# A cross-attention and mixture-of-experts block: short runs in memory, weight reloads one step ahead, a running sum on VectorE, values' product two steps behind the scores

## The chip, the cores and the metric

The kernel runs on one core of a Trainium2 chip. A core has TensorE (PE in the profile; the loading of its stationary operand is PEld), VectorE (DVE), ScalarE (ACT), GpSimd (POOL) and SyncE (SP), and 16 DMA engines that all queues share. SP and POOL issue the DMAs here. The metric is the device time in microseconds; smaller is better. The figure for a kernel is the median of its timed runs; one further execution is recorded by the profiler.

## The reference

Four sequences (b = 0 to 3) of 512 rows by 512 columns go through two blocks.

```python
# block 1: per sequence, on layernormed rows
query, key = ctx @ Wq.T + bq, ctx @ Wk.T + bk
x = x + layernorm(x) @ softmax(query @ key.T).T
# block 2, attention: 16 heads of 128 columns
h = rmsnorm(z, ln1_w)                       # z = layernorm(x)
q, k, v = h @ wq, h @ wk, h @ wv
attn = softmax(causal(q @ k.T / sqrt(128)))
z = z + (attn @ v) @ wo
# block 2, experts: 16 experts of width 352, the 6 best of each row, and a shared one of width 704
t = rmsnorm(z, ln2_w)
cw = top6(softmax(t @ gate_w.T)), renormalised
routed = sum over e of cw[:, e] * ((silu(t @ eg[e].T) * (t @ eu[e].T)) @ ed[e].T)
shared = (silu(t @ sg_w.T) * (t @ su_w.T)) @ sd_w.T
out = x + z + routed + shared
```

## The kernel before, in words

**Precision.** Every product keeps about fp32 accuracy by splitting each operand into an fp16 high and low part (`split`, L72: one ScalarE copy and one VectorE subtraction) and adding three fp16 matmuls (`mm3`, L80; the lines L83, L86 and L87 are its three matmuls wherever it is called). A matmul streams up to 512 columns.

**Stages.** Block 1 for b = 0 and most of b = 1 comes first (about 0 to 85 us of the trace). Then the main loop (L780) goes over 64 heads, one head to a step n, in the order of `path` (L768): two neighbouring sequences take the same pair of heads after each other, so that one load of weights serves both. Block 1 of the later sequences is spread over the steps (`step`, L837 to L841). The loop ends near 1020 us; the shared expert, the 16 routed experts and the gathering of their rows follow.

**A step n of the loop.** `queries` (L637) makes q and k of head n, `values` (L623) makes v for a pair of heads, `scores` (L654) makes the four row blocks of the causal scores with 128, 256, 384 and 512 columns. Each block goes to VectorE (mask and maximum, L671), ScalarE (exponential with sum, L673), VectorE (reciprocal), and then through `split` into the tile `pn`. A DMA transpose on SP's queue (`flip`, L90 and L680) turns `pn` into the tile `pt` in SBUF. `attend` (L682) multiplies `pt` with v. It is called for head n - LAG, and LAG is 1. `project` (L695) multiplies the result with wo when a pair of heads is through, and adds to x2. When the last pair of a sequence is through, `route1` to `route3` (L485, L532, L587) choose the experts; the rows are scattered to the experts' places by 24 indirect DMAs a sequence on POOL's queue (`scatter`, L464). `pace` (L456) is a small POOL copy that reads the newest result of `attend` or of the shared expert, so that POOL doesn't run ahead with its scatters.

**Where order is decided.** The functions are called in the order above, but a scheduler places the instructions on each engine; a tile pool with a fixed number of buffers makes a new tile wait for the old one's last reader. Within one engine, POOL and SP among them, instructions run in the order so placed, and a waiting instruction holds up all behind it.

**Weights.** Sequence 0's pass loads fp32 weights, splits them, uses them, and writes the fp16 pair to DRAM scratch (`wqk_d`, `wv_d`, `wo_d`; 512 KB each, 4 KB to a partition). Later passes reload from there: `fetch` (L407) issues the reload on POOL's queue (L414) in the step in which the weights are used. The tile for a weight has 2 buffers.

**Tiles for the transposed scores.** `pt` is 8 blocks of 512 columns (8 KB a partition), of which the causal triangle fills 20 blocks of 128; the pool `ht` holds two. In `attend` the block row k of v meets the columns from 128k on:

```python
for k in range(NT):
    mm3(pv[:, k * P:], [(vt[:, k, 0, hl], vt[:, k, 1, hl], pt[:, 2 * k, k * P:],
                         pt[:, 2 * k + 1, k * P:])], start=k == 0, stop=k == NT - 1)
```

Of the kernel before, what the change touches and what calls it, by code (L numbers as in the profile page):

```python
# [24 lines left out]
G = 8  # L25
# [24 lines left out]
LAG = 1  # L50
# [5 lines left out]
def xattn_moe_block_kernel(ctx: ExitStack, tc: tile.TileContext, x, xT, ctxT, wqkx, bqk, ln1, ln2,  # L56
# [23 lines left out]
    def mm3(o, terms, start=True, stop=True, hold=None):  # L80
# [7 lines left out]
        return ins  # L88

# [42 lines left out]
    hid_d = [dram.tile([P, NT, D], F32, name=f"hid_d{b}") for b in range(B)]  # L132
    x1_d = [dram.tile([P, NT, D], F32, name=f"x1_d{b}") for b in range(B)]
    wqk_d = [dram.tile([P, 2048], F16, name=f"wqk_d{h}") for h in range(H)]
    wv_d = [dram.tile([P, 8 * GW], F16, name=f"wv_d{g}") for g in range(G)]
    wo_d = [dram.tile([P, 2 * HG * D], F16, name=f"wo_d{g}") for g in range(G)]
    xs_d = dram.tile([ROWS, 2 * D], F16, name="xs_d")
    r_d = [dram.tile([P, NT, D], F32, name=f"r_d{b}") for b in range(B)]
# [30 lines left out]
    ht = bpool("ht")  # L169
# [9 lines left out]
    def ctx_load(b):  # L179
        t = stg.tile([P, 1024], F32, tag="st", name="ct32").rearrange("p (c s) -> p c s", c=CC)  # L180
        feed(b).dma_start(t, ctxT[b])
        return t
# [21 lines left out]
    def xattn(b):  # L204
        ct32 = ctx_load(b) if b else ct0

        def turned(j):
            t = (stg if b else wg).tile([P, 1024], F32, tag="st" if b else "wo", name="xT32")
            feed(b).dma_start(t, xT[b, j])
            return t  # L210
# [5 lines left out]
        if b == 0:  # L216
            nc.sync.dma_start(ln1b, ln1.partition_broadcast(P))
            for nm, src in (("wqk0", wqk[0]), ("wv0", wv[0])):
                t = vp.tile([P, NT, 2, GW], F16, tag="vt", name=f"{nm}_st")
                early_st[nm] = t.rearrange("p t a d -> p (t a d)").bitcast(F32)  # L220
                nc.sync.dma_start(early_st[nm], src)
# [20 lines left out]
        def wide(nm):  # L242
            return (ap_ if b else ht).tile([P, 2 * C, S], F16, tag=nm if b else "pt", name=f"{nm}{b}")
# [88 lines left out]
        for t in range(NT):  # L332
# [6 lines left out]
            q.dma_start(x1_d[b][:, t, :], xv)  # L339
# [15 lines left out]
            if b >= 2:  # L355
                q.dma_start(hid_d[b][:, t, :], hd)
# [37 lines left out]
    def shared_pool():  # L394
# [5 lines left out]
        for j in range(0, C * 2 * SI, 1024):  # L400
            pieces.append((shw[:, :, j:min(j + 1024, C * 2 * SI)], sgu[:, j:min(j + 1024, C * 2 * SI)]))
        for j in range(0, 6 * D, 1024):
            pieces.append((sdw[:, :, j:j + 1024], sd[:, j:j + 1024]))

    held, partner, seen = {}, {}, set()

    def fetch(b, g, pool, tag, n, src, scr, nm):  # L407
        if held.get(nm, (None,))[0] == (b, g):
            return held.pop(nm)[1]
        w = pool.tile([P, 2, n], F16, tag=tag, name=f"{nm}_{b}")  # L410
        if (b, g) in partner:
            held[nm] = partner[b, g], w
        if nm in seen:
            nc.gpsimd.dma_start(w.rearrange("p a n -> p (a n)"), scr)  # L414
# [5 lines left out]
        else:  # L420
            st_ = stg.tile([P, 1024], F32, tag="st", name=f"{nm}_st")
            q = nc.sync if nm == "wqk1" else nc.gpsimd
            ins = q.dma_start(st_[:, :n], src)
# [5 lines left out]
        ins = (nc.sync if nm == "wqk0" else nc.gpsimd).dma_start(scr, w.rearrange("p a n -> p (a n)"))  # L429
# [10 lines left out]
    def shared_weights():  # L440
# [6 lines left out]
        if pieces:  # L447
            dst, src = pieces.pop(0)
            n = src.shape[1]
            st_ = stg.tile([P, 1024], F32, tag="st", name="shst")[:, :n]  # L450
            pin(nc.gpsimd.dma_start(st_, src))
# [842 lines left out]
```

## Time and profile before

| | |
|---|---|
| Median of the timed runs | 1773.08 us (1766.79 to 1774.21, 3 runs) |
| The profiled execution: its own time | 1762.41 us |
| its span from first to last instruction | 1760.7 us |
| mean granted TensorE clock | 0.993 |
| TensorE busy | 1708.6 us, 97% of the span |
| VectorE, ScalarE, GpSimd busy | 63%, 47%, 28% |
| DMA: SP's queue, POOL's queue | 39.9% and 25.5% of 16 engines' span |

The page lists busy times, the granted clock, the DMA queues and the costliest groups of instructions; a row "A <- B: us, times, longest" of the waits says how long engine A stood idle before an instruction and which event ended that. A row of the timeline gives start, duration, engine, line, operation and tiles, and in square brackets the idle time before it. Matmuls overlap, so a matmul's pace is read from the distance between two starts (0.215 us at 512 columns, 0.056 at 128), not from its duration (0.38 us).

### The profile page before, as it was taken

The numbers are of one execution on the slowest core, as the hardware profiler recorded it, in microseconds if no ns is written. First come the engines' busy times: TensorE is split into PE (matmuls) and PEld (weight loads), VectorE is DVE, ScalarE is ACT, GpSimd is POOL, SyncE is SP. The second block draws the span as 40 slices with busy tenths as digits, with TensorE's granted clock in tenths as the row PEclk, the third lists the DMA queues.
The fourth block names the chain that finished last, engine by engine and source line by source line (L and its number), as shares of the span: only waits on it lengthen the run. The fifth ranks groups of instructions, "written<-read, shape, count | busy, mean of one in ns | idle before, by whom it ended". The sixth has DMA issues, their size and how long they took to land. (4 is left out here: it accounts for less than half of the span.)

```text
span 1760.7 us, 27659 instructions
## 1 busy us (share of the span) xinstructions
PE 1708.6 (97%) x9919; PEld 932.9 (53%) x9919; DVE 1116.2 (63%) x2766; ACT 829.3 (47%) x1711; POOL 485.1 (28%) x614
## 2 busy tenths in 40 slices
PE   7899999999998999999999999999999999999998
PEld 3555556565654555556555544455555555555553
DVE  6787877787785676776667647544434344356755
ACT  4565655565643545454445422344544445444431
POOL 5524212240255242121113454300000000034654
PEclk9999999999999999999999999999999999999999
DMA  7787867575687787556547653755554546589866
GB/s 246 181 205 184 225 150 192 122 196 118 138 183 187 163 177 179 120 120 118 111 104 132 140 155 128 247 173 148 150 173 137 154 143 163 154 228 254 221 198 213
DMA packets 392212, 296.24 MB, mean 168 GB/s; under 512 B 334880, under 2 KB 335136, under 8 KB 391296
## 3 DMA queue, kind: packets, MB, share of 16 engines
q1 hardware_dynamic: 353360, 159.87, 39.9%
q0 software_dynamic: 38704, 134.51, 25.5%
q8 instruction: 80, 1.31, 0.3%
q14 instruction: 68, 0.56, 0.1%
HBM read 124.81 MB, written 88.94 MB: 121 GB/s over the span
## 5 line engine op out<-in xcount | busy, mean ns | idle before, releaser
L1169 POOL DMA_INDIRECT yg<-y_d,yrc x96 | 109.9, 1145 | 505.2 <-PE u L87 426.0
L673 ACT ACTIVATE pe<-pe,bnm 128x128 f32<-128x128 f32 (+3 forms) x256 | 142.5, 557 | 161.5 <-DVE bnm L671 161.3
L83 PE MATMUL qk<-hT,wqk 128*128 128x512 f16 (+1 forms) x520 | 196.4, 378 | 9.1 <-DMA wqk<-wqk_d 5.5
L86 PE MATMUL qk<-hT,wqk 128*128 128x512 f16 (+1 forms) x520 | 196.5, 378 | 0.0
L87 PE MATMUL qk<-hT,wqk 128*128 128x512 f16 (+1 forms) x520 | 196.3, 377 | 0.0
L74 DVE SCALAR_TENSOR_TENSOR pn<-pe,brc,pn 128x128 f16<-128x128 f32 (+3 forms) x256 | 148.1, 590 | 21.3 <-ACT pn L73 18.0
L671 DVE CUSTOM_DVE_ANT_0 pe<-sc,causal 128x128 f32<-128x128 f32 (+3 forms) x256 | 117.0, 485 | 66.9 <-PE sc L668 65.9
L73 ACT ACTIVATE pn<-pe,brc 128x128 f16<-128x128 f32 (+3 forms) x256 | 133.5, 553 | 34.1 <-ACT pe L673 17.8
L83 PE MATMUL v<-wv,hT 128*128 128x256 f16 x512 | 139.8, 273 | 0.9 <-DMA hT<-hh 0.9
L87 PE MATMUL v<-wv,hT 128*128 128x256 f16 x512 | 139.7, 273 | 0.0
L86 PE MATMUL v<-wv,hT 128*128 128x256 f16 x512 | 139.7, 273 | 0.0
L83 PE MATMUL g<-xT,wt 128*128 128x384 f16 (+2 forms) x384 | 127.3, 331 | 0.0
L86 PE MATMUL g<-xT,wt 128*128 128x384 f16 (+2 forms) x384 | 127.2, 331 | 0.0
L87 PE MATMUL g<-xT,wt 128*128 128x384 f16 (+2 forms) x384 | 127.2, 331 | 0.0
L1058 ACT ACTIVATE hT_e<-hf 128x384 f16<-128x384 f32 (+3 forms) x96 | 51.1, 532 | 133.6 <-DVE hf L1072 133.2
L83 PE MATMUL y<-dt,hT_e 128*128 128x512 f16 (+1 forms) x288 | 109.4, 380 | 0.0
L87 PE MATMUL y<-dt,hT_e 128*128 128x512 f16 (+1 forms) x288 | 108.9, 378 | 0.0
L86 PE MATMUL y<-dt,hT_e 128*128 128x512 f16 (+1 forms) x288 | 108.9, 378 | 0.0
L73 ACT ACTIVATE qkt<-qk 128x512 f16<-128x512 f32 x128 | 75.1, 587 | 70.7 <-PE qk L87 70.5
L705 DVE SCALAR_TENSOR_TENSOR x<-wo,x 128x512 f32<-128x512 f32 x128 | 87.2, 685 | 33.3 <-PE wo L87 32.9
L467 POOL DMA_INDIRECT xs_d<-h2p,slotu x96 | 98.7, 1028 | 28.3 <-issue 27.1
L74 DVE SCALAR_TENSOR_TENSOR qkt<-qk,qkt 128x512 f16<-128x512 f32 x128 | 87.5, 684 | 18.3 <-ACT qkt L73 15.2
(333 smaller groups left out, 4041.5 us busy)
## 6 DMA issues: line engine op xcount, KB each, us to landing
y_d<-yt SPq DMA_DIRECT2D x96, 256.0 KB, 2.8
est<-in_ew_dram SPq DMA_DIRECT2D x32, 704.0 KB, 6.2
est<-in_ed_dram SPq DMA_DIRECT2D x16, 768.0 KB, 4.7
wqk<-wqk_d POOLq DMA_DIRECT2D x20, 512.0 KB, 5.0
wqk_d<-wqk POOLq DMA_DIRECT2D x15, 512.0 KB, 4.0
wqk_st<-in_wqk_dram POOLq DMA_DIRECT2D x14, 512.0 KB, 6.4
xs_d<-causal POOLq DMA_DIRECT2D x16, 384.0 KB, 5.6
wv<-wv_d POOLq DMA_DIRECT2D x10, 512.0 KB, 5.7
```

The lines of the kernel that those rows point to most:

```text
L73: return (nc.scalar.activation(hi, src, AF.Copy, scale=scale), nc.vector.scalar_tensor_tensor(lo, src, scale, hi, ALU.mult, ALU.subtract))
L74: nc.vector.scalar_tensor_tensor(lo, src, scale, hi, ALU.mult, ALU.subtract))
L83: ins = nc.tensor.matmul(o, lh, rh, start=start and j == 0, stop=False)
L86: nc.tensor.matmul(o, lh, rl, start=False, stop=False)
L87: ins = nc.tensor.matmul(o, ll, rh, start=False, stop=stop and j == n - 1)
L467: ins = nc.gpsimd.indirect_dma_start(out=xs_d, out_offset=bass.IndirectOffsetOnAxis(ap=slotu[:, tt, k:k + 1], axis=0), in_=h2ps[tt], in_of ...
L671: nc.vector.tensor_tensor_reduce(pe, ps[:, :w], causal[:, S - w:], -1.0, 3e38, ALU.add, ALU.min, nm)
L673: nc.scalar.activation(pe, pe, AF.Exp, bias=nm, scale=-1.0, accum_out=sm)
L705: nc.vector.scalar_tensor_tensor(x2[:, t, :], ps, 1.0 / (VS * WS), x2[:, t, :], ALU.mult, ALU.add)
L1058: nc.scalar.activation(hT[:R, ic, :w], hf, AF.Copy)
L1169: nc.gpsimd.indirect_dma_start(out=yg, out_offset=None, in_=src, in_offset=bass.IndirectOffsetOnAxis(ap=idx[:, tt, k:k + 1], axis=0))
```

## The change

1. `LAG` is 2: `attend` of a head is called two steps after its `scores`. The pool `ht` has 3 buffers. The tile `pt` is packed: 20 blocks of 128 columns, so a flip writes one stretch. `attend` goes over pairs of row blocks instead, with 18 matmuls of 256 or 128 columns in place of 12 of 512, 384, 256 and 128. The last two heads are attended in step 64.
2. `fetch` has a mode `early`: after the queries of step n, the reloads of the weights of step n + 1 are issued (q/k and v), and wo's in the step that attends the pair's last head. `pace` is placed behind them.
3. `runs` cuts every plain DMA of those tensors in pieces; the scratch tensors and four inputs are laid out as [piece, partition, run] with runs of 1 KB in scratch and 2 KB in the inputs.
4. The running sum over experts in `route2` (four additions a sequence) goes from GpSimd to VectorE.
5. Around these: block 1 of b = 0 keeps one tile in `hpool` in place of `ht`; steps 1 to 5 take three pieces of b = 1's block 1 instead of steps 0 to 5 two; the early part of the shared expert takes 2 chunks to a tile, and two chunks, one, and three are placed around the last heads.

```diff
-LAG = 1
+RUN = 256
+LAG = 2
...
+    def runs(q, o, i):
+        blocks = [v.rearrange("p (q n) -> p q n", q=w.shape[0]) if len(v.shape) == 2 else v.rearrange("q p n -> p q n")
+                  for v, w in ((o, i), (i, o))]
+        return q.dma_start(*blocks)
...
-    wqk_d = [dram.tile([P, 2048], F16, name=f"wqk_d{h}") for h in range(H)]
+    def rows_d(nm, b):
+        return dram.tile([NT, D // RUN, P, RUN], F32, name=f"{nm}{b}")
+
+    def weights_d(nm, i):
+        return dram.tile([2048 // (2 * RUN), P, 2 * RUN], F16, name=f"{nm}{i}")
...
-    ht = bpool("ht")
+    ht = bpool("ht", LAG + 1)
...
-    def fetch(b, g, pool, tag, n, src, scr, nm):
+    def fetch(b, g, pool, tag, n, src, scr, nm, early=False):
+        if early and nm not in seen or soon.get(nm) and early:
+            return
         if held.get(nm, (None,))[0] == (b, g):
-            return held.pop(nm)[1]
-        w = pool.tile([P, 2, n], F16, tag=tag, name=f"{nm}_{b}")
+            return None if early else held.pop(nm)[1]
+        w = soon.pop(nm, None)
+        if w is None:
+            w = pool.tile([P, 2, n], F16, tag=tag, name=f"{nm}_{b}")
+            if nm in seen:
+                zz["load"] = runs(nc.gpsimd, w.rearrange("p a n -> p (a n)"), scr)
+        if early:
+            soon[nm] = w
+            return
...
-        if "rrs" in zz:
-            after(ins, zz["rrs"])
+        for k in ("rrs", "load"):
+            if k in zz:
+                after(ins, zz[k])
...
-            nc.gpsimd.tensor_tensor(nx[:, :, sft:], cs[:, :, sft:], cs[:, :, :E - sft], ALU.add)
+            nc.vector.tensor_tensor(nx[:, :, sft:], cs[:, :, sft:], cs[:, :, :E - sft], ALU.add)
...
-        pt = pts[b, h] = ht.tile([P, 2 * NT, S], F16, tag="pt", name="pt")
+        pt = pts[b, h] = ht.tile([P, NT * (NT + 1), P], F16, tag="pt", name="pt")
...
-            flip(pt[:, :2 * (t + 1), tl], pn)
+            flip(pt[:, t * (t + 1):(t + 1) * (t + 2), :], pn)
...
-        for k in range(NT):
-            mm3(pv[:, k * P:], [(vt[:, k, 0, hl], vt[:, k, 1, hl], pt[:, 2 * k, k * P:],
-                                 pt[:, 2 * k + 1, k * P:])], start=k == 0, stop=k == NT - 1)
+        for t in range(0, NT, 2):
+            for k in range(t + 2):
+                q = max(k, t)
+                o = pv[:, q * P:(t + 2) * P].rearrange("p (n q) -> p n q", q=P)
+                first = q * (q + 1) + 2 * k
+                phi, plo = (pt[:, first + a:first + a + 2 * (t + 1 - q) * (q + 1) + 1:2 * (q + 1), :] for a in range(2))
+                mm3(o, [(vt[:, k, 0, hl], vt[:, k, 1, hl], phi, plo)], start=k == 0, stop=k == t + 1)
...
-    for n in range(NH + LAG + 1):
+    for n in range(NH + 2):
...
+            if n + 1 < NH:
+                b, h = heads[n + 1]
+                wqk_of(b, h, True)
+                if h % HG == 0:
+                    wv_of(b, h // HG, True)
         m = n - LAG
...
-            for ic in range(3 * (n - NH), 3 * (n - NH) + 3):
...
+            hs0 = chunks(*((3, 6) if n > NH else (0, 2)))
...
-        if 0 <= m < NH:
-            b, h = heads[m]
+        for i in [m] * (0 <= m < NH - LAG) + [NH - 2, NH - 1] * (n == NH):
+            b, h = heads[i]
             attend(b, h)
             if h % HG == HG - 1:
                 ready.append((b, h // HG))
+                wo_of(b, h // HG, True)
+        if n == NH:
+            chunks(2, 3)
...
-            step(1, 2)
+            step(1, 3 * (n > 0))
```

## The prediction, made before the changed kernel had run

> **What bounds the kernel now.** I read the busy shares first, then TensorE's waits, then the timeline around the longest waits and POOL's timeline at the same moments.
>
> ```profile
> span 1760.7 us, 27659 instructions
> ## 1 busy us (share of the span) xinstructions
> PE 1708.6 (97%) x9919; PEld 932.9 (53%) x9919; DVE 1116.2 (63%) x2766; ACT 829.3 (47%) x1711; POOL 485.1 (28%) x614
> ```
>
> TensorE is busy 97% of the span, and its matmuls follow each other at the pace of their columns. So only its pauses can be won, and every pause that the change adds is lost. The waits of the whole run:
>
> ```profile
> engine line waited for: us in total, times, longest us
> PE av L83 <- DMA pt<-pn: 16.9, 10, 3.9
> PE xm L83 <- DMA ptp<-pn: 9.8, 2, 5.8
> PE qk L83 <- DMA wqk<-wqk_d: 5.5, 1, 5.5
> PE u L1081 <- DVE hf L1072: 3.9, 2, 2.1
> PE qk L83 <- DMA hT<-hh: 3.6, 2, 3.2
> ```
>
> The first and third rows lie in the main loop and are what parts 1 and 2 of the change aim at: values waiting for transposed scores, and one q/k weight that came late. The second and fifth belong to the start. Now the late weight on TensorE:
>
> ```profile
> 542.92 0.38 PE L668 MATMUL sc<-qkt,qkt 128*128 128x512 f16 x1
> 548.81 0.61 PE L83 MATMUL qk<-hT,wqk 128*128 128x512 f16 x1 [5.51 <-DMA wqk<-wqk_d]
> 549.21 0.63 PE L86 MATMUL qk<-hT,wqk 128*128 128x512 f16 x1
> 549.64 0.63 PE L87 MATMUL qk<-hT,wqk 128*128 128x512 f16 x1
> 550.07 0.63 PE L83 MATMUL qk<-hT,wqk 128*128 128x512 f16 x1
> ```
>
> After the pause starts are 0.43 us apart where 0.215 is usual: half pace. It lasts to 554.0, which costs 2.6 us more. The same follows the longest wait for scores (3.91 us, ending at 970.0): half pace to 972.8, 1.2 us. No other wait of the loop, the longest of them 2.48 us, is followed by it. On POOL's queue at that time:
>
> ```profile
> 537.35 1.28 POOL L467 DMA_INDIRECT xs_d<-h2p,slotu  x1 [0.30 <-issue]
> 538.93 0.96 POOL L467 DMA_INDIRECT xs_d<-h2p,slotu  x1 [0.30 <-issue]
> 539.89 0.60 POOL L414 DMA_DIRECT2D wqk<-wqk_d  x1
> ```
>
> The reload is issued at 539.89, three microseconds before TensorE wants it, behind ten scatters that POOL had been issuing since 525.7, about 1.27 us each.
>
> **LAG 2 and the packed triangle.** TensorE's columns stay the same: 512 + 384 + 256 + 128 = 1280 before, 2 x 128 + 128 + 3 x 256 + 128 = 1280 after, three matmuls each. Instructions rise from 12 to 18 per head, 384 in all. A 128-column matmul starts 0.056 us after the last and a 256-column one 0.109, so cutting 256 in two costs 3 ns; 384 x 3 ns = **+1 us**. The moving operand now steps over blocks of 128, which the trace has nowhere. It can't gain, as the columns are the same; at worst each block costs like a matmul of its own, 64 x 12 x 3 ns = 2 us. I take nothing, as all rows here go by columns.
>
> For the wait I compare, head by head, two things. The latency from the last 512-column score matmul to the landing of the last flip, in the trace, is 14.5 us in the median and 23.2 at most. The cover is the matmul work that stands in TensorE's order between those scores and the head's first value matmul, columns at 0.422 ns. It is 11.0 to 24.0 us before, under 14.5 in fourteen heads; in the changed order it is 13.2 for the first head, 17.9 for the second, and 19.5 to 40 for all others. With the old latencies only one head past the first falls short, by 0.8 us. I leave 1 us: **16.9 - 1 = 15.9 us gone, and 1.2 of half pace**.
>
> What comes later in its place? Each `attend` moves with its ScalarE and VectorE split, then `project`, behind one more head. Two covers shrink. The time between the end of q/k and the first scores falls to 2.3 to 3.8 us in about twenty heads (4.8 was common); the old q/k latencies (1.4 us usual, up to 6.8 early) laid against it give **+2 us** in two heads, early. The first `project` of heads 2 and 3 gets 1.0 us after its values, against a split of 0.58 + 0.68 us: **+0.5 us**. At the end, the last wo matmul stands 14.9 us before the router's matmuls of sequence 3, against 19.9 before; the chain between (norm, split, four flips) took 18.0, of which the last flip took 7.7 where 2.9 is the median. So 0 to 3.1 us; I take **+1.5**. A flip now also waits for `attend` of three heads ago; no flip is behind that, as the third buffer goes with the longer lag.
>
> **Reloads a step ahead.** In POOL's new order the reload that stalled stands before the ten scatters, and the next one, behind twenty of them, is wanted about 37 us of matmul work later. Buffers are free when it is issued, since the tile's last reader is a head back. So **5.5 + 2.6 us go**. POOL's idle time ahead of L414 (82 us for wo, 58 for q/k), in which all its queue stood, shrinks too; nobody on the critical path had felt it otherwise.
>
> **Short runs.** 71 of POOL's copies go from 128 to 512 runs, 95 from 128 to 256, and SP's likewise at the start. Two costs. First, issue: the one POOL copy of 128 x 4 runs is L215, the usual one L414.
>
> ```profile
> L215 POOL DMA_DIRECT2D xt<-in_x_dram x2: 788/812/837, 136.6 to 347.6; - x2
> L414 POOL DMA_DIRECT2D wqk<-wqk_d x20: 528/546/597, 444.0 to 958.8; - x20
> ```
>
> So 71 x 0.27 = 19 us, and 95 x 0.09 = 9 us if it goes by runs: 28 us of POOL's time over 1000. The Trainium skill ("DMA: Bandwidth & Descriptors", "Anatomy of one DMA") says descriptor generation on this path is small and that many can be emitted before the increment shows; by that the cost is nothing. I take the row. Neither is on the path: POOL is busy 28%, and the reloads now have a head's time. If that cover were gone, each would cost 0.27 us, about 10 us for 40 reloads.
>
> Second, the DMA engines. In the trace a 2 KB packet takes 84 ns and a 4 KB one 159, so 9 ns and 37 ns per KB; four runs of 1 KB would take 183. Then 72 x 128 x 24 ns / 16 = 14 us of each engine, with the 2 KB pieces about 20 us in 1000: 2 points on a DMA share of 0.5 to 0.87. The same page ("Why small descriptors are slow") speaks against the edit more mildly, with some 3 cycles a packet beside 32 for 1 KB: 7% in place of 15%. Both ends are hidden behind flips with 5 us of new slack. Better spread in DRAM could also shorten transfers (4 KB packets of POOL's queue average 217 ns against a median of 159). I take zero, with -3 to +3 us for the start, where loads stand on the path.
>
> **Running sum.** 16 additions leave POOL (0.27 to 0.29 us) for VectorE, where the same size takes 0.155 (L957): 2.5 us on an engine at 63%, in the router's chain, which has a step to spare. Zero. The other rearrangements (tile pools, chunks) keep TensorE's work; b = 1's first value product gets 1 us more of matmuls ahead of its 4 us wait at 72 us: **-1**.
>
> **The sum.** -15.9 - 1.2 - 5.5 - 2.6 - 1 = -26.2; +1 + 2 + 0.5 + 1.5 = +5. Net -21. Against the profiled execution, 1762.4 - 21 = 1741. The median of the timed runs lies 10.7 us above that execution; I carry this over: **1752 us**, faster by 1.2%.
>
> **The rivals.**
> - *The main case*, 0.64: 1752, within 1742 to 1762 for the open ends above and a measurement scatter of some 7 us.
> - *The scores' chain stretches* to fill the new time, because VectorE (79% busy from 88 to 528 us) serves heads in another order: half of the waits for flips and some q/k waits stay. Gain 8 to 10: about 1764. For it: VectorE is the next busiest there. Against: its work is the same. 0.14.
> - *More is won*: pauses, half pace and clock between 88 and 1012 us add up to 33 us over the columns' own time, and transfers at the start get quicker: 33 + 4 gone, 1736. 0.10.
> - *Slower*: the DMA engines become the bound. If a 1 KB run costs what a 2 KB one does (84 ns), a 4 KB row takes 336 ns in place of 159: 72 x 128 x 177 / 16 = 102 us more on each engine, most of it in the first half, where the share is already 0.72. It decides once flips take 6 us longer, since most covers are near 21 us or more. At 8 us longer, half of 64 heads wait 1.5 us: +48 - 26, so 1795. Against: the trace's fixed part of a packet is 9 ns. 0.12.
> - *The change doesn't do what it says* is excluded in its core: the new order shows the longer lag and the earlier reloads.
>
> A measurement of this kernel can tell about 0.5% from no change, so faster is under 1764.2 and slower over 1782. Faster: 0.64 + 0.10 and under half of the second case, less some tail of the first: 0.76. Same 0.13, slower 0.11. Range: 1737 to 1770 leaves out the slower case and part of the third.
>
> **What would show it.** Right: the row av <- pt near 1 us, no row wqk <- wqk_d, the clock at 1.00 from 528 to 572, 10,303 matmuls, POOL's reload issues near 0.81 us, DMA share in the loop within 3 points. Wrong: a row sc <- qkt or wo <- ao of over 5 us, flips landing much over 3.7 us in the median, or longer pauses before 90 us.

## The result and the profile after

The changed kernel is slower: 1.007 times the kernel before, 95% interval 1.0045 to 1.0095. The medians are 1779.12 us (9 runs) and, beside it, 1769.19 us (9 runs). The forecast was 1752 us. The profiled execution took 1777.59 us, against 1762.41 before.

The busy times of its page (share of a span of 1775.6 us, number of instructions), to be laid beside those shown of before:

```profile
PE 1716.6 (97%) x10303; PEld 964.0 (54%) x10303; DVE 1129.2 (64%) x2782; ACT 832.0 (47%) x1713; POOL 516.2 (29%) x597
```

TensorE has the 10,303 matmuls foreseen, the span is 15 us longer, and no engine's share has moved by more than a point. So it is TensorE's pauses again, and the half pace that follows some of them. TensorE's waits of the changed kernel, whole run (us in total, times, longest; some lines have moved: L84 was L83, L738 was L705):

```profile
PE sc L695 <- DVE bnm L700: 8.9, 4, 3.7
PE wo L84 <- DVE x L738: 7.4, 5, 2.4
PE lg L569 <- DMA h2T<-h2p: 3.2, 2, 3.0
...
PE sc L695 <- ACT qkt L74: 2.6, 2, 1.7
...
PE av L84 <- DMA pt<-pn: 1.7, 2, 1.4
```

Both rows that the change aimed at went as forecast: values' waits for scores fell from 16.9 to 1.7 us, and the late q/k weight has no row. In their place stand rows that the kernel before had not, or hardly: scores that wait for VectorE's mask and maximum of earlier scores (`bnm`) or for ScalarE's half of q/k (`qkt`), and wo products that wait for VectorE's addition to x. The first and the third of them are waits for a PSUM bank, the memory that a matmul writes: `scores` takes its banks from a pool of three and `project` shares two with `attend`, and a bank comes free when VectorE has read it. So the next question is what VectorE was doing. Its waits between 88 and 1110 us, first of the kernel before, then of the changed one:

```profile
DVE pe L671 <- PE sc L668: 65.9, 48, 8.5
DVE x L705 <- PE wo L87: 32.9, 49, 2.3
...
DVE tid L615 <- POOL w L614: 3.8, 2, 3.1
...
DVE nb L352 <- POOL r L347: 2.8, 3, 1.6
```

```profile
DVE x L738 <- PE wo L88: 46.9, 57, 1.4
...
DVE pe L700 <- PE sc L697: 8.7, 17, 1.8
DVE nb L363 <- POOL r L358: 8.6, 6, 3.7
DVE tid L644 <- POOL w L643: 8.3, 2, 5.6
```

Before, VectorE waited 65.9 us for TensorE's scores: it was ahead there. After, that is 8.7 us, and its waits for POOL, at instructions that have nothing to do with the scores, have grown from 18.9 to 35.0 us in all (among them `tid`, the token index, and `nb`, of the row norm). VectorE runs in order; while it stands before `tid` or `nb`, the reading of score banks behind them stands too. VectorE is hardly busier than before (64% against 63%), and it waits longer for wo products (46.9 us against 32.9). What went is its lead at the scores.

To say where the time lies I add up, stage by stage, TensorE's start-to-start distances less its columns at 0.4219 ns ("time over the columns"). It is 70.4 us before and 87.5 after: 59.1 and 62.5 up to the last value product, 3.4 and 14.0 from there to the first routed expert, 7.9 and 11.0 in the rest. Sorted by kind instead, 46.1 us before and 57.6 after lie in distances with a pause, 9.3 and 12.3 in matmuls at half pace; the 18 smaller matmuls of `attend` cost the 1 us that was forecast (0.6 and 1.6).

### The profile page after: what moved, and what is told of

The parts are those of the page before. It is cut to its first block, busy times and chain, and to the rows that moved or that the text cites. A ratio compares the mean times of both kernels' runs of the same rounds, so it can differ in the third digit from the quotient of the medians.

```text
span 1775.6 us, 28409 instructions
## 1 busy us (share of the span) xinstructions
PE 1716.6 (97%) x10303; PEld 964.0 (54%) x10303; DVE 1129.2 (64%) x2782; ACT 832.0 (47%) x1713; POOL 516.2 (29%) x597
## 3 DMA queue, kind: packets, MB, share of 16 engines
q1 hardware_dynamic: 358992, 159.87, 39.6%
q0 software_dynamic: 38960, 134.51, 25.3%
## 4 chain that ended last, share of the span: by engine, by line
PE 47%; DMA 5%; POOL 3%; issue 3%; DVE 3%; ACT 1%; another core or an unknown queue 0%; SPq 0%; POOLq 0%; DVEq 0%; ACTq 0%
PE g L87 3%; PE g L84 3%; PE g L88 3%; PE y L84 3%; PE y L87 3%; PE y L88 3%; PE u L87 2%; PE u L88 2%; PE u L84 2%; PE qk L87 2%; PE qk L88 2%; PE qk L84 2%; POOL yg L1217 1%; PE u L1129 1%; PE u L1130 1%
## 5 line engine op out<-in xcount | busy, mean ns | idle before, releaser
L84 PE MATMUL qk<-hT,wqk 128*128 128x512 f16 (+1 forms) x520 | 195.4, 376 | 3.6 <-DMA hT<-hh 3.0
L75 DVE SCALAR_TENSOR_TENSOR pn<-pe,brc,pn 128x128 f16<-128x128 f32 (+3 forms) x256 | 148.3, 592 | 23.3 <-ACT pn L74 21.1
L84 PE MATMUL v<-wv,hT 128*128 128x256 f16 x512 | 140.7, 275 | 2.1 <-DVE qkt L75 1.3
L84 PE MATMUL g<-xT,wt 128*128 128x384 f16 (+2 forms) x384 | 127.3, 331 | 0.5 <-DMA xT<-xs_d 0.5
L700 DVE CUSTOM_DVE_ANT_0 pe<-sc,causal 128x128 f32<-128x128 f32 (+3 forms) x256 | 115.0, 484 | 12.3 <-PE sc L697 11.9
L738 DVE SCALAR_TENSOR_TENSOR x<-wo,x 128x512 f32<-128x512 f32 x128 | 87.1, 688 | 53.6 <-PE wo L88 46.9
L84 PE MATMUL y<-dt,hT_e 128*128 128x512 f16 (+1 forms) x288 | 109.5, 380 | 0.0
L84 PE MATMUL wo<-wo,ao 128*128 128x512 f16 x256 | 97.0, 379 | 7.4 <-DVE x L738 7.4
```

The source lines that it names most:

```text
L75: nc.vector.scalar_tensor_tensor(lo, src, scale, hi, ALU.mult, ALU.subtract))
L84: ins = nc.tensor.matmul(o, lh, rh, start=start and j == 0, stop=False)
L700: nc.vector.tensor_tensor_reduce(pe, ps[:, :w], causal[:, S - w:], -1.0, 3e38, ALU.add, ALU.min, nm)
L738: nc.vector.scalar_tensor_tensor(x2[:, t, :], ps, 1.0 / (VS * WS), x2[:, t, :], ALU.mult, ALU.add)
```

## The experiments

All were timed in five rounds in turn with the kernel before, on one chip. The four parts (short runs; earlier reloads; running sum; longer lag with packed triangles and the chunks' new places) can be switched singly; the scheduler places all instructions for each kernel. Line numbers of these kernels differ a little from those of the changed one (L711 for L695, L716 for L700, L757 for L738, L76 for L75).

| kernel | ratio to before, 95% interval | over the columns in its trace, us: to the last value / to the first expert / rest |
|---|---|---|
| before; again, as e2_null | 1.000; 1.000 [0.9967, 1.0032] | 59.1 / 3.4 / 7.9; 59.1 / 3.5 / 6.7 |
| lag alone | 1.0026 [1.0004, 1.0047] | 63.3 / 7.1 / 3.7 |
| earlier reloads alone | 1.0006 [0.9981, 1.0031] | 61.2 / 4.3 / 9.0 |
| short runs alone | 1.0113 [1.0066, 1.0160] | 79.6 / 3.5 / 7.0 |
| sum alone | 0.9998 [0.9976, 1.0020] | 55.3 / 3.3 / 5.8 |
| all four (the changed kernel) | 1.0070 [1.0045, 1.0095] | 62.5 / 14.0 / 11.0 |
| all but short runs | 1.0065 [1.0037, 1.0092] | 58.6 / 13.5 / 4.5 |
| all but lag | 1.0065 [1.0044, 1.0085] | 64.2 / 5.2 / 13.0 |
| all but sum | 1.0060 [1.0038, 1.0081] | 62.0 / 7.6 / 13.7 |
| all but earlier reloads | 1.0045 [1.0025, 1.0066] | 62.2 / 9.2 / 13.3 |
| all, loads ahead of stores | 1.0095 [1.0055, 1.0134] | 82.9 / 5.3 / 5.3 |
| all, products on VectorE | 1.0000 [0.9975, 1.0025] | 60.8 / 4.7 / 10.5 |
| all, chunks together | 1.0038 [1.0009, 1.0067] | 70.4 / 7.0 / 5.8 |
| lag, sum, products, loads first | 0.9963 [0.9937, 0.9990] | 59.5 / 5.3 / 6.8 |
| lag, sum, products | 0.9975 [0.9951, 0.9998] | 49.2 / 8.1 / 4.7 |
| sum, products, lag of 1 | 0.9952 [0.9931, 0.9974] | 54.5 / 3.2 / 6.4 |
| lag, sum, products, counts, chunks | 0.9958 [0.9932, 0.9985] | 50.0 / 8.8 / 7.5 |
| lag, sum, products, no low halves | 1.0046 [1.0015, 1.0078] | 66.3 / 8.8 / 14.1 |
| lag of 1, sum, products, no low halves | 1.0152 [1.0111, 1.0194] | 84.3 / 3.4 / 15.3 |

The last column is one execution each. Its third number moves between 3.7 and 15.3 us though nearly all kernels have the same code there, so no cause is read from it.

### One part undone

```diff
# all but short runs
-        return q.dma_start(*blocks)
+        return q.dma_start(o, i)          # and DRAM tiles [P, NT, D], [P, 2048]
# all but lag
-LAG = 2
+LAG = 1                                   # and pt of 8 x 512, 2 buffers, 12 matmuls, old chunks
# all but sum
-            nc.vector.tensor_tensor(nx[:, :, sft:], ...)
+            nc.gpsimd.tensor_tensor(nx[:, :, sft:], ...)
# all but earlier reloads
-        if early and nm not in seen or soon.get(nm) and early:
+        if early:
             return
```

All but short runs:

> The changed kernel with the short runs undone (rows and weights in memory as before, copies of 128 and 256 rows again), all else changed. Theory A1, the short runs: POOL's copies take 0.2 us longer to issue each, so POOL serves VectorE late, VectorE stands in front of such an instruction, score banks and wo banks come free late, and TensorE pauses. Then the ratio to the kernel before is 0.993 or below (about 1757 us), the rows sc <- bnm and wo <- x fall from 8.9 and 7.4 us to under 3 each. Theory A2, the order: the longer lag itself places work on VectorE and POOL so that these pauses arise. Then the ratio stays at 1.005 to 1.009 and both rows remain over 5 us. Theory A3, the running sum on VectorE: also 1.005 to 1.009.

All but lag:

> The changed kernel with the lag of 1, the unpacked score tile, two of them, and the old places of the shared chunks; short runs, earlier reloads and running sum stay. Theory A2 (order): the pauses sc <- bnm and wo <- x go, the pauses av <- pt of 17 us come back; ratio 0.995 to 1.000. Theory A1 (short runs): the pauses for VectorE stay and av <- pt comes back too; ratio 1.010 to 1.020 (after's 1.007 and 16 us more, less overlap). Theory A3 (running sum): the same as A1.

All but sum:

> The changed kernel with the 16 additions of the running sum back on POOL. Theory A3: the sum puts VectorE behind POOL's earlier steps and makes it stand; then the ratio falls to 0.995 to 1.000 and sc <- bnm and wo <- x to under 4 us each. Theories A1 and A2: the stands of VectorE that were seen are at other instructions (the row norm's nb, the token index, the staged weights), so the ratio stays at 1.005 to 1.009.

All but earlier reloads:

> The changed kernel with the reloads where they were asked for before, a head later; all else changed. By the prediction's step 8 us come back (one late q/k weight): ratio 1.010 to 1.013, with a row wqk <- wqk_d of about 5 us. If the earlier reloads are themselves what makes POOL late for VectorE, the rows sc <- bnm and wo <- x fall to under 4 us each and the ratio to 1.000 to 1.004. If the longer lag alone already shields the q/k weight, the ratio stays at 1.005 to 1.009 without such a row.

Measured: 1.0065, 1.0065, 1.0060 and 1.0045; all four intervals overlap that of the changed kernel. None of the four is the cause by itself. A1 falls: without the short runs the kernel is as slow, and sc <- bnm is still 6.1 us, wo <- x 4.8, and 5.7 have come as av <- x. VectorE's waits for POOL, which A1 put down to the longer issues, are 37.2 us without the short runs and 35.0 with them. A2 falls as it was put: without the lag the pauses for VectorE do go (sc <- bnm 0.2 us) and av <- pt comes back (15.0 us), as A2 said, yet the time stays. A3 falls. Of the earlier reloads, the last of the expectations fits: no row of a late q/k weight came back and the time did not rise. In the traces with and without this part every compute engine's instructions, and POOL's DMA issues, stand in the same order, so it moved nothing, and in both the reload of q/k is issued some 15 us before the first scatter (at 534.7 and 536.9 us). The removal of the lag suggests that two sets of pauses of like size stand in for each other; it does not show it, as that kernel also keeps the short runs at a lag of 1, which are dear by themselves (next section).

### One part alone, and the kernel before once more

The edits are those above, the other way round.

> All four parts undone: instruction for instruction the kernel before, on every engine and in the same order. It sets the scale of the others: every theory expects a ratio of 1.000 within 0.003, and its trace is a second look at the kernel before. Where this trace has other waits than the first, of that size is the scatter between two looks at one program; I expect values' waits for scores between 12 and 20 us, the late q/k weight again, and TensorE's time over its columns between 65 and 80 us.

> The kernel before with the lag of 2, the packed triangles and the new places of the shared chunks alone. The prediction's step: 17 us of waits for scores go and 4 come: ratio 0.991 to 0.994. Theory B (the wait moves: with the longer lag VectorE has no reserve over TensorE, so each time it stands before POOL or a late weight, TensorE stands too, for a score or a wo bank): ratio 0.998 to 1.007, rows sc <- bnm and wo <- x over 8 us together, VectorE's own wait for scores (65.9 us before in the loop) under 20. Theory C (each of the four parts alone moves the placed work a little and costs 0.1 to 0.2%): 1.000 to 1.003.

> The kernel before with the reloads a step earlier alone. The prediction's step: one wait of 5.5 us and its half pace go: ratio 0.994 to 0.997. Theory B (VectorE without reserve through the lag): here the lag is as before, so the same 0.994 to 0.998. Theory C: the order of POOL and VectorE moves (some 350 and 1150 lines of their orders differ) and new waits come in the place of the old one: 0.999 to 1.004, the row wqk <- wqk_d gone all the same.

> The kernel before with the short runs alone. The prediction's step: nothing on the path: ratio 0.998 to 1.001. Theory B: the longer issues of POOL (28 us in all) reach TensorE only where VectorE has no reserve; at the lag of 1 it has, so 0.999 to 1.002. Theory C: 1.001 to 1.004. If the short runs slowed the flips, values' waits for scores would rise from 16.9 us to over 25 and the ratio to over 1.005.

> The kernel before with the running sum alone on VectorE. The prediction's step: nothing, 0.998 to 1.001. Theory C (every shift of the order costs something): 1.001 to 1.003. If the sum on VectorE makes VectorE stand before POOL's two products behind it, over 1.003.

The kernel before against itself gave 1.000, and its second trace differs from the first by 1.1 us over the columns in all, while single waits scatter more (av <- pt 14.4 against 16.9, the late weight 2.3 against 5.5).

*The lag alone* is no gain: 1.0026 where the prediction's step would give 0.991 to 0.994. Theory B's expectations all fit: the ratio, the new rows and VectorE's own wait. TensorE's waits in this kernel:

```profile
PE sc L711 <- DVE bnm L716: 8.9, 2, 6.1
...
PE sc L711 <- ACT qkt L75: 7.4, 1, 7.4
PE av L85 <- DVE x L757: 4.8, 1, 4.8
...
PE av L85 <- DMA pt<-pn: 0.6, 1, 0.6
```

The wait for transposed scores is gone (14 to 17 us before, 0.6 now), and four pauses, 21.1 us together, have come. One of them from near: TensorE's values wait for a bank of `project`, and what VectorE does meanwhile (rows of the timeline of the kernel with the lag alone, for TensorE, VectorE, ScalarE and POOL):

```profile
192.31 0.27 PE L85 MATMUL av<-pt,vt 128*128 128x256 f16 x1 [4.85 <-DVE x L757]
```

```profile
190.44 1.23 DVE L76 SCALAR_TENSOR_TENSOR wv<-wv_st,wv 128x1024 f16<-128x1024 f32 x1 [6.74 <-ACT wv L75]
191.58 0.68 DVE L757 SCALAR_TENSOR_TENSOR x<-wo,x 128x512 f32<-128x512 f32 x1
```

```profile
189.35 1.06 ACT L75 ACTIVATE wv<-wv_st 128x1024 f16<-128x1024 f32 x1 [6.89 <-DMA wv_st<-in_wv_dram]
```

```profile
176.77 0.99 POOL L94 DMA_DIRECT2D wv_st<-in_wv_dram  x1
191.96 0.54 POOL L94 DMA_DIRECT2D wv_d<-wv  x1 [14.19 <-DVE wv L76]
```

POOL issues the fp32 load of a v weight at 176.77; it is used at 189.35. ScalarE stands before it 6.89 us, VectorE 6.74, and the addition that would free TensorE's bank is the next instruction behind. The two longest of the four pauses have the same form. The one of 7.4 us ends at 409.7, behind a late wo weight; the one of 6.1 us ends at 661.9, behind POOL's running sum, which itself came after a load that POOL waited 9.95 us for:

```profile
407.94 1.23 DVE L76 SCALAR_TENSOR_TENSOR wo<-wo_st,wo 128x1024 f16<-128x1024 f32 x1 [7.09 <-ACT wo L75]
660.78 0.17 DVE L625 COPY rcs<-rcs 128x8 f32<-128x8 f32 x1 [10.23 <-POOL rcs L626]
```

Such long pauses cost more than their length. After the one at 192.31 TensorE's matmuls of 256 columns start 0.21 us apart where 0.109 is usual:

```profile
193.28 0.42 PE L89 MATMUL av<-pt,vt 128*128 128x256 f16 x1
193.49 0.42 PE L85 MATMUL av<-pt,vt 128*128 128x256 f16 x1
```

All four are followed by half pace, 7.8 us together by the distances between starts; in the two traces of before half pace in the loop cost 3.7 and 4.5 us.

The kernel before has the same v weight late: in its second trace ScalarE waits 3.28 us for it and VectorE 2.56, but there VectorE has read the four blocks of scores ahead of the split and TensorE's own wait there, 2.0 us, is for `pt`. With the longer lag TensorE does not stop for `pt` there; what it meets is a late weight in front of VectorE. Over the loop VectorE's wait for scores falls from 59.7 us to 9.7, and its waits for POOL rise from 18.6 to 44.3 (the second trace of before, and the lag alone). The reload that the change wanted earlier has moved ahead of the scatters here too (534.56 us, the first scatter at 549.25), with the lag alone.

*The earlier reloads alone* are worth nothing (1.0006), and for a plain reason. One of TensorE's wait rows with that part alone, and POOL's queue:

```profile
PE qk L85 <- DMA wqk<-wqk_d: 8.2, 1, 8.2
```

```profile
542.25 0.96 POOL L509 DMA_INDIRECT xs_d<-h2p,slotu  x1 [0.30 <-issue]
543.20 0.61 POOL L94 DMA_DIRECT2D wqk<-wqk_d  x1
```

The reload still stands behind the ten scatters. Asking for it earlier in the program did not move it ahead of them; the scheduler placed it where it was. All engines' instructions stand in the same order as in the kernel before, so the 8.2 us, beside 5.5 and 2.3 in the two traces of before, are scatter. Theory C's guess of the ratio held, its guess that this row would be gone did not.

*The short runs alone* cost 1.1%, 20 us. This is the greatest single effect of the study, and the prediction had it at zero. TensorE's waits with them alone:

```profile
PE av L85 <- DMA pt<-pn: 25.8, 12, 5.6
...
PE qk L85 <- DMA wqk<-wqk_d: 6.9, 1, 6.9
```

At the lag of 1 values wait 25.8 us for scores (14.4 and 16.9 before). The busy times by stretch, from 88 to 640 us, show what became slower; first the kernel before in its second trace, then the short runs alone (length; busy us and instructions of PE, PEld, DVE, ACT, POOL; granted clock; DMA share; GB/s):

```profile
88.00:640.00 552.00, 541.66 (x3356) 308.87 (x3355) 421.93 (x1188) 300.62 (x681) 173.26 (x234) 0.99 0.72 172
```

```profile
88.00:640.00 552.00, 520.56 (x3132) 294.60 (x3131) 401.97 (x1110) 286.74 (x651) 181.36 (x219) 0.98 0.73 164
```

The DMA engines are as busy as before but move 164 GB/s in place of 172, and POOL needs 8 us more for fewer instructions. Fewer bytes are in part a result, since the whole loop runs later. Nor have POOL's copies filled the engines. The rows of POOL's queue, before and with the short runs alone (packets, MB, share of 16 engines' span):

```profile
q0 software_dynamic: 38704, 134.51, 25.5%
```

```profile
q0 software_dynamic: 38960, 134.51, 25.2%
```

The packets are nearly as many as before. Those of 4 KB are 30,784 before and 32,832 with the short runs, with a median of 159 ns in both, and none of 1 KB is on this queue. So copies of 512 runs did not become four times the packets here, and the queue took each engine 449 us before and 448 with them. SP's queue, which does have 1 KB packets now (5,632), took 2 to 3% more.

The flips share these engines. Of those in this stretch whose landing the trace resolves (some 90 of 140), the middle one lands 4.1 us after its issue before and 4.2 with the short runs, but the slowest quarter takes over 5.9 us before and over 7.2 with them, the slowest tenth over 7.3 and 8.5. First-time weights come later too: ScalarE stands before them 34.4 us between 88 and 700 us, against 26.1 and 28.7 in the two traces of before. So a tail grew in the busy half of the loop, and values at a lag of 1 had no cover for it, as the last of the expectations had it (over 25 us, over 1.005). Why it grew is open: the longer issues are one candidate, but the edit also moved some 350 of TensorE's matmuls and 180 of VectorE's instructions to other places, and no run parts the two. With the lag of 2 and the rest, the same runs cost nothing that could be measured (1.0070 with, 1.0065 without), which fits: there av <- pt is 1.7 us. The effects don't seem to add: singly they make 1.4% (0.26 + 0.06 + 1.13 - 0.02), together 0.7%.

*The sum alone*: 0.9998, as the prediction's step had it.

### What VectorE waits for

```diff
# loads ahead of stores: the scratch store of a weight is emitted after the next weight's load
             ins = runs(q, st_[:, :n], src)
+            flush_store(ins)
# products on VectorE (four statements in route2 and route3)
-            nc.gpsimd.tensor_tensor(w4[:, t * K:(t + 1) * K, :], o4[:, t], ..., ALU.mult)
+            nc.vector.tensor_tensor(w4[:, t * K:(t + 1) * K, :], o4[:, t], ..., ALU.mult)
# chunks together (and none behind the last values)
-            hs0 = chunks(*((3, 6) if n > NH else (0, 2)))
+            hs0 = chunks(*((3, 6) if n > NH else (0, 3)))
```

> The changed kernel in which POOL issues the next weight's first load ahead of the store of the weight before it (before, each load stood in POOL's queue behind a store that waits for VectorE's split, so loads and splits ran one after the other). Theory B, VectorE stands before late weights and TensorE then waits for banks that VectorE frees: VectorE's waits for wo, wv and wqk (29.7 us of 88 to 1110 us in the changed kernel) fall to under 15, sc <- bnm and wo <- x lose the pauses at 107 and 398 us, and the ratio falls by 0.003 to 0.005 to 1.002 to 1.004. If TensorE's pauses have another cause, VectorE's waits fall and the ratio stays at 1.005 to 1.009.

> The changed kernel with the router's remaining products (counts by mask, slots, gates, expert numbers) on VectorE in place of POOL, so that VectorE does not stand before POOL's scatters there. Theory B: the waits tid <- w (8.3 us), slot and cw <- w go, and with them the pauses of TensorE at 563, 679 and 1014 us, some 5 us: ratio 1.003 to 1.005; some 20 products of 0.2 to 0.6 us more on VectorE give 1 to 2 us of it back at most. If VectorE's own load is what it lacks, the ratio rises to 1.008 to 1.012.

> The changed kernel with the third chunk of the shared expert of sequence 0 back beside the first two, ahead of the last values, as the kernel before had it. If the chunk's new place makes the pauses between the loop's end and the first expert (14.0 us over the columns in the changed kernel, 3.4 before, 7 in the kernel with the lag alone), they fall by half or more and the ratio to 1.003 to 1.005. If they come of the last two heads being attended in one step, of the longer lag itself, the ratio stays at 1.006 to 1.008.

> The kernel before with the longer lag, the running sum and the router's products on VectorE, and loads ahead of stores; neither the short runs nor the earlier reloads. Theory B: the lag's own gain of 15 us shows once VectorE stands less: ratio 0.993 to 0.998. If each shift of the placed work costs as much as it gives, 0.999 to 1.004.

*The products.* 1.0000 [0.9975, 1.0025] against 1.0070 [1.0045, 1.0095]: the intervals don't meet. That is more than the 0.2 to 0.4% expected from the pauses that I could point to, and it is the one edit to the changed kernel whose gain is clear of noise: it takes back what the change cost. VectorE's waits for POOL between 88 and 1110 us, in the changed kernel 35.0 us in eight rows, are now 14.5 us in four, of which the larger two are:

```profile
DVE h L545 <- POOL h2p L80: 6.9, 3, 6.0
DVE nb L376 <- POOL r L371: 5.5, 6, 2.7
```

*Loads ahead of stores* did not help (1.0095; the interval overlaps that of the changed kernel). VectorE's waits for the three weights, which were to fall from 29.7 to under 15 us, are 28.8 (wo 14.0 where it was 11.3), and the loop to the last value got 20 us longer. The edit did not do what it was meant to do, and by the traces it also moved some 440 of TensorE's matmuls and 115 of VectorE's instructions to other places. So it says nothing on whether late loads matter.

*The chunks*: 1.0038 where the middle stage fell from 14.0 to 7.0 us over the columns, as expected. But the intervals overlap, the lag alone, with the chunks in their new places, has 7.1 there, and a later kernel with the chunks together has 8.8. Not settled.

*The best guess* is faster than both kernels, 0.9963, within theory B's range; but it changes the products and the loads along with the lag, and the next runs show that the lag has no part in it.

### Does the lag matter for the products, and does it gain at all?

> The kernel before with the longer lag, the running sum and the router's products on VectorE, without the short runs, the earlier reloads and the loads ahead of stores. If putting loads first cost time also here (1.0095 against 1.007 in the changed kernel), this is faster than the last guess: ratio 0.992 to 0.995. If the loads' order was of no account, 0.995 to 0.998.

> The kernel before with the running sum and the router's products on VectorE, at the lag of 1 and with nothing else. Theory B1, VectorE's stands before POOL cost TensorE time only where the longer lag has spent VectorE's reserve: ratio 0.999 to 1.002, though VectorE's waits for POOL's products go. Theory B2, they cost TensorE as much at either lag: 0.992 to 0.996.

> The first of this call with two things more: POOL's addition to the running counts of the experts on VectorE too (TensorE's rank matmuls waited for it 4.5 us behind POOL's scatters), and the third chunk of sequence 0 beside the first two. If the wait for the counts and the chunk's place each cost what their waits show (3 to 5 us and 2 to 5 us), the ratio is 0.003 to 0.005 under the first of this call: 0.988 to 0.992. If they only move waits, it is the same as the first within 0.002.

The edits: short runs and earlier reloads off, sum and products on VectorE, at either lag; in the third, `m2` (the running counts) by `nc.vector` as well, and the chunks together.

At the lag of 1 the products gain 0.46% (0.9998 to 0.9952), at the lag of 2 as much (1.0026 for the lag alone, 0.9975, though there the sum goes along); neither pair of intervals meets. So B1 falls and B2's range fits: VectorE's reserve at the lag of 1 did not protect the kernel from POOL's products; they were on the path of the kernel before too. One way in which they were is plain in the trace. POOL's queue at the lag of 1, first with the sum alone, then with the products moved:

```profile
528.38 1.13 POOL L509 DMA_INDIRECT xs_d<-h2p,slotu  x1 [0.18 <-issue]
...
541.82 0.61 POOL L94 DMA_DIRECT2D wqk<-wqk_d  x1
```

```profile
526.83 0.58 POOL L94 DMA_DIRECT2D wqk<-wqk_d  x1 [2.26 <-PE qk L89]
...
530.08 1.09 POOL L509 DMA_INDIRECT xs_d<-h2p,slotu  x1 [0.31 <-DVE cw L658]
```

With the products away the very q/k reload that the change wanted earlier is issued 15 us earlier, ahead of the scatters, and its pause (7.2 us with the sum alone) is gone. What else went, VectorE's waits for `tid`, `cw` and `slot`, was 5.9 and 6.4 us in the two traces of the kernel before. The edit also gives the rest another order (some 470 of TensorE's matmuls stand elsewhere), so how the gain divides is not shown.

And the lag: with the products moved, 0.9975 at a lag of 2 and 0.9952 at 1. Their intervals overlap; a gain of 0.9%, which 16 us would be, is excluded. Of the expectations for the lag of 2 the second fits (0.995 to 0.998, the loads' order of no account). In the two traces av <- pt goes from 19.9 us to 1.0, and among what comes (lag of 2) are:

```profile
PE av L85 <- DVE x L757: 5.2, 2, 4.9
...
PE lg L585 <- DMA h2T<-h2p: 2.0, 2, 1.7
PE rk L642 <- POOL macc L644: 1.9, 1, 1.9
```

The stage from the last value to the first expert has 8.1 us over the columns, against 3.2 at the lag of 1; every kernel with the lag of 2 has 4.7 to 14.0 there, those with 1 have 3.2 to 5.2. Counts and chunks on top of it made 0.9958, which can't be told from the 0.9975 without them, as the second expectation had it.

### The waits for late weights taken away

In both, the low half of a first-time attention weight is zero, set by VectorE, instead of being split off:

```diff
-        split(w[:, 0], w[:, 1], st_[:, :n], WS)
+        nc.scalar.activation(w[:, 0], st_[:, :n], AF.Copy, scale=WS)
+        nc.vector.memset(w[:, 1], 0.0)
```

> Lag of 2 with running sum and products on VectorE (0.9975), with one thing left out: the low halves of the attention weights that are loaded for the first time are set to zero on VectorE in place of being split off, so that VectorE waits for no late weight (ScalarE, which makes the high halves, still does). Theory B: at the lag of 2 VectorE's stands of 26 us before late weights hold TensorE up by some 7 us (4.9 at 189, 1.7 at 404 us); they go: ratio 0.993 to 0.995, a gain of 0.003 to 0.005. If the stands cost TensorE nothing, 0.996 to 0.999.

> The same left out at the lag of 1 with running sum and products on VectorE (0.9952). Theory B: at the lag of 1 VectorE's stands of 26 us before late weights lie beside work that TensorE has, its waits being for scores (av <- pt 19.9 us): a gain of 0.002 at most, ratio 0.993 to 0.996. If the stands cost TensorE as much at either lag, the gain is the same as in the run with the lag of 2.

Measured: 1.0046 and 1.0152, slower by 0.7 and 2.0% than the same kernels with the split. VectorE's waits for ScalarE before these weights are gone, ScalarE's own stay (41.9 and 24.3 us). By the traces some 400 and 760 of VectorE's instructions and 770 and 1730 of TensorE's matmuls have come to stand elsewhere, and the kernel at the lag of 1 has a pause of 9.3 us for the transposed `hh` where the others have at most 3.5. Of the 39 us that it lost over the columns, 14 are half pace. Neither expectation held. The test did not isolate what it was to isolate, and theory B's part about late weights stays argued from traces, not shown. What the pair does show is that an edit which takes work away can cost 2%; the new placement is the likely reason.

## Why the prediction was wrong, point by point

- *What bounds the kernel*: right. TensorE stayed at 97%, and what changed is pauses and the half pace behind them.
- *The waits for scores, 15.9 us gone*: right in the trace to within a microsecond (1.7 left, 1 forecast), alone (0.6 left) and together. The method (latency of the chain against the cover in TensorE's order) held, and so did the 1 us for smaller matmuls.
- *"What comes later in its place?"*: this is the step that failed. It answered +2, +0.5 and +1.5 us, by laying TensorE's shrunk covers against latencies of the old trace. Measured in the changed kernel: 8.9 + 7.4 + 2.6 for scores' banks, wo banks and q/k, 3.2 for the router's transposes and 2.3 of half pace after it. With the lag alone it was 21.1 us of new pauses and 7.8 of half pace, where the step had 4 in all. The step asked when TensorE's operands are ready and not when its banks are free. VectorE frees them in order, and 65.9 us of VectorE's waits before were waits for scores: time in hand, of which 8.7 were left. A late weight or a busy POOL in front of VectorE then reached TensorE, as the rows at 192, 408 and 661 us show with the lag alone. That kernel came to 1.0026 where this step's sum gave some 0.993. That the lost lead is why is read from traces; the runs that were to remove the late weights did not settle it.
- *The reload, 5.5 + 2.6 us gone*: its row is gone in the changed kernel. The place in POOL's order was read rightly too, but it is not the work of this part: the longer lag alone moves the reload ahead of the scatters, the products on VectorE do so at the lag of 1, and the earlier reloads alone leave it behind them, with a wait of 8.2 us. In time the part is worth nothing alone, and its removal did not make the changed kernel slower.
- *Short runs, "Neither is on the path: POOL is busy 28%"*: wrong, and the biggest term alone: 1.1% against zero. The issue cost itself was well sized. The rows of before (546 ns) and of the changed kernel:

```profile
L94 POOL DMA_DIRECT2D wqk<-wqk_d x20: 751/770/852, 445.5 to 955.2; - x20
```

  0.77 us for 0.81 forecast. By the Trainium skill ("DMA: Bandwidth & Descriptors", "Anatomy of one DMA"), which has descriptor generation on this path as small, it would have stayed near 0.55; the row decided rightly. But an average of 28% says nothing of an in-order queue at the moments when VectorE or TensorE stand behind it. Whether the issues or the new placement cost the 1.1% is open. In the changed kernel the term does not show (1.0070 with, 1.0065 without), so it is not what made that kernel slow.
- *DMA engines*: the share was right (39.6 and 25.3% of the span against 39.9 and 25.5), but not for the reason given. The 14 to 20 us were reckoned for four packets of 1 KB in place of one of 4 KB; POOL's queue kept its packets of 4 KB (32,832, none of 1 KB), so neither that cost nor the milder one came there. The slower rival falls with the same row. Flips that land later in the first half are to be seen with the short runs alone, but as 1.3 us in the slowest quarter, where it asked for 6 us; the changed kernel is slow by another way.
- *Running sum, zero*: right (0.9998 alone).
- *The rivals*: the second, that VectorE serves heads in another order, was nearest, but it still kept 8 to 10 us of gain and had scores, not banks, come late. None had the loss: POOL's work and late weights reaching TensorE through VectorE.
- *What would show it*: the signs that the prediction named for being right came (av <- pt at 1.7 us, no late q/k weight, the clock at 1.00 from 528 to 572 us, 10,303 matmuls, issues of 0.77 us, the DMA share), and sc <- qkt and wo <- ao stayed under 5 us (the flips' landings are not resolved in this trace). The signs followed the waits that the step had thought of; the loss came under other names.
- *Where the gain went*, then: in the traces, the 16 us of the lag went into 21 us of waits for banks and q/k (lag alone), with half pace behind them, and 4 us (lag alone) to 11 us (all four) in the stretch from the loop's end to the first expert. Shown by runs is that the lag gives nothing at three pairs (alone; with all else; with the products moved), and that POOL's products cost 0.5 to 0.7% in the three kernels in which they were moved. Open is how the rest divides between late first-time weights and mere placement.

## What to carry to other kernels

When a longer lag or prefetch takes away a producer's wait, look at the engine that frees the consumer's PSUM banks: list what that engine waits for, in order, and ask what is behind it, because its time in hand is what the change will spend. A small product on an in-order queue can be worth more than the pipelining: four statements moved from POOL to VectorE (with the running sum, which gave 0.9998 alone) gave 0.9952 [0.9931, 0.9974], the whole change 1.0070. And where a scheduler places the work, measure each part alone and beside a copy of the old kernel, and compare the orders in the traces: one edit here moved hundreds of instructions that it doesn't name, another moved none.

## What had not been expected of the hardware

- POOL's issue of a copy grew with the number of its runs: 0.55 us at 128 runs, 0.77 us at 512. The packets of its queue did not shrink with the runs: 30,784 of 4 KB became 32,832, and none was of 1 KB.
- With the short runs alone the flips' middle landing stayed (4.1 and 4.2 us) while their slow tail grew, from 5.9 to 7.2 us at three quarters.
- Half pace came after the long pauses of TensorE: in the lag-alone kernel all four of 2.8 to 7.4 us cost 1.5 to 2.4 us more each. In the second trace of before, pauses of 2.0 and 2.3 us did so too, where the first had none under 3.9 in the loop.
- TensorE's time over its columns in two traces of one program (before) agreed within 1.1 us in all, while single rows moved by 2 to 3 us (16.9 and 14.4; 5.5 and 2.3).
